# Where an exp tile is put: places chosen by the kernel's own order account, with new times for adding transfers

## The chip, the cores and the metric

The kernel runs on one core of a Trainium2 chip. The metric is the device time of one execution in microseconds (us), from launch to end, as the median of several runs. The profile is one further execution with the hardware profiler on; its span runs from the first to the last instruction.

## The reference, cut to what matters

Everything is float32. Eight images of 256 channels and 32 x 32 pixels go through three parts.

```python
# part 1: attention of 1024 pixel queries over 1426 pooled and convolved keys, 8 heads of 32
k_map, v_map = kv_w @ groupnorm(x)
ks, vs = layernorm(pooled(k_map)), layernorm(pooled(v_map))     # levels 32x32, 16x16, 11x11, 5x5
attn = softmax(q @ k.T * SCALE)
x = x + proj(mix(attn @ v))
# part 2: self-attention over the 1024 tokens, one head of 256
t = t + softmax(q @ k.T * SCALE) @ v
# part 3: eight experts of three 256 x 256 layers on every token, summed by gates
t = t + sum_e gate[e] * (relu(bn(relu(bn(n @ W1[e])) @ W2[e])) @ Wo[e] + bo[e])
```

In parts 1 and 2 the softmax is taken without a row maximum: exp of the scaled scores, the weighted values, the column sums, one division. A check at the end falls back to a slower path if a sum has left its bounds.

## The kernel before, in words

**Stages.** `attention` (L914) computes parts 1 and 2 together, `experts` (L2178) part 3. In the profiled execution the first lasts until about 1925 us. Within `experts` the order of the instructions is written out by hand, but for the gates. Within `attention` it comes from `Flow` (from L671): the kernel keeps an account of its own, with a clock for each engine (`now`), for each tile the time at which it is ready (`ready`) and last read (`read`), and costs by operation (`cost`, L724). Every instruction goes through `note` (L766), which ties it behind the last one written for its engine, so that the order in which Python writes the instructions is the order of each engine's queue. All instructions appear under line 671 in the profile, since they are issued through `Flow.Engine`.

**What is written when.** The main loop at the end of `attention` goes over 8 images, 2 channel halves, 2 query halves and 11 key chunks of 128 keys, 352 steps; the 12th chunk, of 18 keys, is handled once an image. A step writes `scores` (L1538) and then `values` (L1548) of the step before. All other work is in generators (`spawn`, L846), each with a rank, which yield what they need next: an engine and tiles. `step` (L883) resumes those for which `runnable` (L856) holds. For PE that is as long as there is credit, or as long as PE's clock is half a microsecond short of `until`, the time at which the scores' PSUM place becomes free by the account. DVE work is let in when DVE's clock is at most 4.0 us ahead of PE's if its tiles are ready, and otherwise when they will be ready within 1.5 us of PE's clock. `finish` (L896) resumes generators by the earliest start, whatever the credit, until a condition holds.

**The life of an exp tile.** `scores` writes 16 matmuls in the array's small tiles into the one PSUM tile `sc` (4 banks), takes a tile of the tag `pt` (128 x 4 x 512, 1 MiB; six places in SBUF), and writes one exp from `sc` to `pt`. `values` multiplies it with the values into `pv`. Of each two neighbouring chunks the odd exp tile is then added to the even one by an adding DMA that GpSimd (POOL) issues (`add`, L1593). The generator `sums` (L1600) adds each such pair to the first pair of its unit on DVE, in two halves, and at the end multiplies the first pair with ones for the column sums. So an odd tile's place is free when its add has landed, an even one's after the DVE sum, and the first pair's after the last matmul of the unit of 11 steps. Two of the six places serve the first image's maps (`first_maps`, L1198) at the start, and one the last image's input in `project` (L1631) at the end.

**Part 2's exp tiles** carry the tag `p1` (128 x 2 x 256, six places). `layer1` (L1695) writes four for each of the 32 query blocks, held back by the count `taken`; `outputs` (L1749) reads them. Small weight tiles in `mix` and `weights1` use the same tag earlier.

**Places before.** `Flow.tile` (L705) asks the tile framework for a tile of a tag with six places; which place it gets is up to the framework's scheduler. Beside it the account keeps a list of six names and replaces the one with the smallest `end`, the later of `ready` and `read` by the account. An instruction's start in the account includes the `ready` of the tile that it writes; a place's end from uses that are not written yet is not known to it.

**Transfers in the account.** `note` gives a DMA 1.0 us for the issue on POOL and 0.4 on another queue, and a landing by `transfer` (L814): a fixed part, its own work by size, and what is left of earlier transfers of its own and of the other queues.

```python
size = 4e-3 * out.shape[0] * out.free_size()          # thousand bytes
lag = self.transfer(engine, end, size * (0.0054 if engine == "POOL" or both else 0.003))
return 1.7 + left[mine] + min(left[mine], left[other]) + self.served - at
```

The functions that the change touches:

Of the kernel before, what the change touches and what calls it, by code (L numbers as in the profile page):

```python
# [8 lines left out]
F32 = mybir.dt.float32  # L9
# [7 lines left out]
P = 128  # L17
# [6 lines left out]
NK = 1426  # L24
# [10 lines left out]
MARGIN = 1.5  # L35
AHEAD = {"DVE": 4.0, "ACT": 2.0, "POOL": 1.0, "SP": 10.0}
NEAR = {"DVE": 1.5, "ACT": 2.0, "POOL": 1.0, "SP": 10.0}
BUFS = {"sm": 2, "sx": 1}
AHEAD3 = 3
PACE2 = 8.0  # L40
# [13 lines left out]
class Kit:  # L54
# [3 lines left out]
        self.nc = nc  # L58
        self.n = 0

    def tile(self, pool, shape, tag, bufs=None):
        self.n += 1
        return pool.tile(shape, F32, tag=tag, name=f"{tag}_{self.n}", bufs=bufs)

    def rstd(self, out, var, eps):
# [592 lines left out]
class Flow:  # L658
# [27 lines left out]
    def __init__(self, tc, kit):  # L686
        nc = tc.nc
        self.tc, self.kit = tc, kit
        self.now = dict.fromkeys(("PE", "DVE", "ACT", "POOL", "SP"), 0.0)
        self.last = {}  # L690
        self.ready, self.read, self.writer, self.reader, self.slots, self.open = {}, {}, {}, {}, {}, set()
        self.pe = self.Engine(self, "PE", nc.tensor)
        self.ve = self.Engine(self, "DVE", nc.vector)
        self.act = self.Engine(self, "ACT", nc.scalar)
        self.pool = self.Engine(self, "POOL", nc.gpsimd)
        self.sp = self.Engine(self, "SP", nc.sync)
        self.threads = []
        self.cut = {}
        self.also = {}
        self.tiled = None  # L700
        self.columns = False
        self.left, self.served = [0.0, 0.0], 0.0
        self.credit, self.port = [0.0, 0.0], 0.0

    def tile(self, pool, shape, tag, bufs=1):  # L705
        t = self.kit.tile(pool, shape, tag, bufs=bufs)
        slots = self.slots.setdefault(tag, [None] * bufs)
        i = min(range(bufs), key=lambda i: self.end(slots[i]))
        self.ready[t.name] = self.end(slots[i])
        slots[i] = t.name  # L710
        if tag in BUFS:
            self.open.add(t.name)
        return t

    def end(self, name):

# [49 lines left out]
    def note(self, engine, op, ins, args, kwargs):  # L766
        aps = [a for a in (*args, *kwargs.values()) if hasattr(a, "tensor") or hasattr(a, "space")]
        out = kwargs.get("out", args[0] if args else aps[0])
        srcs = [a for a in aps if a is not out]
        prev = self.last.get(engine)  # L770
        if prev is not None:
            self.tc.add_manual_dep(
                ins.ins,
                prev,
                mybir.DependencyInfo(mybir.DependencyClass.NoSync, mybir.DependencyReason.DATA),
                reason="program order",
            )
        self.last[engine] = ins.ins.name
        start = self.now[engine]
        names = [n for a in srcs for n in self.keys(a)]  # L780
        outs = self.keys(out)
        for n in (*names, *outs):
            if self.writer.get(n) != engine:
                start = max(start, self.ready.get(n, 0.0))
        for o in outs:
            if self.reader.get(o, engine) != engine:
                start = max(start, self.read.get(o, 0.0))
        cost = self.cost(engine, op, out, srcs)
        if engine == "PE":

            tiling = None if op == "transpose" else self.tiling(srcs)
            if tiling != self.tiled:
                cost += {None: 0.2, "rows": 0.2, "columns": 0.13, "both": 0.2}[tiling]
                self.tiled = tiling

        wide = [a for a in srcs if a.space != PSUM and a.free_size() > 4]
        if "dma" not in op and engine == "POOL" or engine == "DVE" and wide and (len(wide) > 1 or op in ("tensor_scalar", "tensor_copy")):
            start = max(start, self.port)
            self.port = start + cost
        self.now[engine] = end = start + cost  # L800
        lag = 0.15
        if "dma" in op:
            both = out.space == DRAM and srcs[0].space == DRAM
            size = 4e-3 * out.shape[0] * out.free_size() if out.space != DRAM else 4e-3 * srcs[0].shape[0] * srcs[0].free_size()
            lag = self.transfer(engine, end, size * (0.0054 if engine == "POOL" or both else 0.003))
        for n in {*outs, self.key(out)}:
            self.ready[n] = max(self.ready.get(n, 0.0), end + lag)
            self.writer[n] = "DMA" if "dma" in op else engine
        self.open.difference_update(names)
        for n in {*names, *map(self.key, srcs)}:  # L810
            self.read[n] = max(self.read.get(n, 0.0), end + lag)
            self.reader[n] = engine

    def transfer(self, queue, at, work):  # L814

        span = max(0.0, at - self.served)
        self.served = max(self.served, at)
        mine, other = queue == "POOL", queue != "POOL"
        left = self.left
        both = 2 * min(left)  # L820
        done = min(span, both) / 2
        for i in range(2):
            left[i] = max(0.0, left[i] - done - max(0.0, span - both))
        left[mine] += work
        return 1.7 + left[mine] + min(left[mine], left[other]) + self.served - at

    @staticmethod
    def key(a):
# [85 lines left out]
def attention(tc, kit, f, outer, ended, nb, consts, x, t1, t2, hn, bounds, vecs, q_t, kv_t, proj_t, gqk_t, wqk, wqkv, vecs1, w1_d, w1c, gate_d, wrc, vecs2, bnvec, w2_d, h2d, between, pre, held):  # L914
# [6 lines left out]
    with ExitStack() as ctx:  # L921
# [71 lines left out]
        def mix():  # L993
# [46 lines left out]
            yield act(wa)  # L1040
            f.act.activation(wa, wa, AF.Exp)
            yield ve(wa)
            rs = T(wp, [P, 2], "wars")
            f.ve.tensor_reduce(rs, wa, AX.X, ALU.add)
            f.ve.reciprocal(rs, rs)
# [18 lines left out]
            for c in range(2):  # L1064
                f.pe.matmul(
                    ps[:, c * C : (c + 1) * C], lhsT=bdt[:, c, :], rhs=pjw[:, c, :], start=True, stop=True
                )
            yield ve(ps)
            raw = T(l1, [P, 2, C], "s")
            f.ve.tensor_copy(raw, ps.rearrange("p (c q) -> p c q", c=2))  # L1070
            for c in range(2):
# [28 lines left out]
        def ve(*tiles):  # L1100
            return "DVE", tiles, None
# [76 lines left out]
            return dy, dx, max(0, -dy), n - max(0, dy), max(0, -dx), n - max(0, dx)  # L1178


        pmaps = [T(pool_, [P, NK], f"p{i}") for i, pool_ in enumerate((between, work))]
        for t in pmaps:
            f.split(t, 512, HW)
        first, large, whole, pooled, asked, halved = {}, [], [], [], [], []
# [67 lines left out]
        def first_keys(half):  # L1252
# [3 lines left out]
            for m in range(2):  # L1256
# [5 lines left out]
                for i, tap in enumerate((4, 0, 1, 2, 3, 5, 6, 7, 8)):  # L1262
# [7 lines left out]
                        stop=i == 8,  # L1270
                    )
                f.act.activation(acc[:, half * 512 : half * 512 + 512], ps, AF.Identity, bias=db(m, 0))
            large.append(("keys", half))

        def taps(c, s, p, acc, base=0):
# [324 lines left out]
        def sums(n, pairs):  # L1600

            for i in range(1, NKC // 2):
                yield until(lambda: len(pairs) > i)
                for j in range(0, 4, 2):
                    s = pairs[0][:, j : j + 2, :]
                    yield ve(s, pairs[i])
                    f.ve.tensor_tensor(s, s, pairs[i][:, j : j + 2, :], ALU.add)
            yield until(lambda: normalised[0] == n)
            yield pe(pairs[0], tag="sm")
            total = small()  # L1610
            for j in range(4):
                f.pe.matmul(
                    total[DH * j : DH * j + DH, :], lhsT=kit.ones[:, :DH], rhs=pairs[0][:, j, :], start=True, stop=True
                )
            return total

        def normalise(b, c, sl, total, n):
# [12 lines left out]

        def project(b):  # L1631
            if b == nb - 1:
                last = T(work, [P, 2, HW], "pt", bufs=6)
                f.sp.dma_start(last, x[b].rearrange("(k p) n -> p k n", p=P))
            for m in range(2):
# [17 lines left out]
                        f.pool.dma_start(out=t1[b][:, m, sl], in_=xt, accum_op=ALU.add)  # L1653
            if b == nb - 1:
                f.sp.dma_start(t1[b], last)
            projected[0] += 1

        def scale_tokens(src, n):
# [90 lines left out]
        def outputs():  # L1749

            for i in range(4 * nb):
# [23 lines left out]
                for m in range(2):  # L1775
                    for kc in range(8):
# [7 lines left out]
                            stop=kc == 7,  # L1784
                        )
                taken[0] += 1
                yield ve(ps, rec)
                m2 = ps.rearrange("p (m q) -> p m q", m=2)
                f.ve.tensor_tensor(m2, m2, rec[:, None, :].to_broadcast([P, 2, C]), ALU.mult)
# [31 lines left out]
        def weights1():  # L1821
# [76 lines left out]
            wrs = T(wp, [P, 2, NE], "wrs")  # L1898
            yield from centred(cm, wr, NE, wrs)
            f.sp.dma_start(wrc, wrs)  # L1900
            ready.append(True)

        gw, wv = (T(l1, [P, 2, C], tag) for tag in ("gw", "wv"))
# [4 lines left out]
        def experts_ahead():  # L1908

            yield until(lambda: made[0] == nb and key_parts[0] == 3 * nb)  # L1910
            for e, tag in enumerate(("p0", "kt")):
                w = held["w"][e] = T(between, [P, 2, 2, C], tag)
                f.sp.dma_start(w[:, 0], w1c[:, e])
                f.sp.dma_start(w[:, 1], w2_d[:, e])
# [78 lines left out]
        for i in range(len(steps) + 1):  # L1993
            if i < len(steps):
# [12 lines left out]
                if kc == NKC - 1:  # L2007
                    f.finish(lambda: key_parts[0] > 3 * b + 2 and (b, 1) in qs and (b or len(asked) == 4))
                    tail_scores(b)
                else:  # L2010
                    pts[i] = scores(b, c, sl, kc)
                f.step()
            if i and steps[i - 1][3] < NKC - 1:
# [7 lines left out]
                f.finish(lambda: kc1 // 4 in vts[b1])  # L2021
                values(b1, c1, kc1, pts[i - 1], pv)
                if kc1 % 2:
                    add(kc1, pts.pop(i - 1), pts[i - 2])
                    pairs.append(pts.pop(i - 2))
                if kc1 == NKC - 2:
# [725 lines left out]
```

## Time and profile before

| what | value |
|---|---|
| median of 3 runs | 3259.01 us (3258.67 to 3266.59) |
| profiled execution, its time | 3261.05 us |
| its span | 3259.2 us |
| mean granted PE clock | 0.98 |
| exps of part 1 on ACT | 352, 1877 ns each, 660.9 us |
| DVE sums of exp tiles | 320, 391.9 us busy |
| adding DMAs of 1 MiB | 160, 7.7 us from issue to landing (median) |
| adding DMAs of the last 18 keys | 32, 4.4 us |

The engines are PE (matmul), PEld (weight load, beside PE), DVE (VectorE), ACT (ScalarE), POOL (GpSimd) and SP (SyncE, which issues loads and stores). A row of the waits reads "who <- whom: us in total, times, longest"; where a transfer is named, the engine waited for its landing. A time line row gives start, length, engine, line, operation, output <- inputs, form and count, and in brackets how long the engine had been idle and what released it. Numbers are left out of tile names, so `pt` stands for every exp tile of part 1, and `p` for the maps as well as for `p1`. PEclk is the clock that PE was granted, as a share of full speed.

### The profile page before, as it was taken

How to read it: one execution, taken by the hardware profiler on the slowest of the kernel's cores; microseconds unless marked ns; L12 is line 12 of the kernel's file. 1: busy time of each engine (PE TensorE's matmuls, PEld its weight loads, DVE VectorE, ACT ScalarE, POOL GpSimd, SP SyncE). 2: the span in 40 equal slices, each digit the busy share in tenths (PEclk: the TensorE clock that was granted, in tenths of full speed). 3: DMA queues.
4: the chain of work that ended last, by engine and by line, in shares of the span. 5: the costliest groups of instructions: out<-in, count | busy, mean ns of one | idle time of the engine just before them, and what ended most of it. 6: DMA issues, size and time to landing. Idle time of an engine off the chain costs nothing.

```text
span 3259.2 us, 55911 instructions
## 1 busy us (share of the span) xinstructions
PE 3056.5 (94%) x22330; PEld 1789.3 (55%) x22330; DVE 2406.7 (74%) x4117; ACT 1682.6 (52%) x2301; POOL 1240.7 (38%) x1327
## 2 busy tenths in 40 slices
PE   8778799999979989989999999999999999999998
PEld 4322234334325334424333356777888888888887
DVE  5886786987877888969754544447888887777776
ACT  4566566666645657657665533333333334444443
POOL 3211413224222232232121112007655667777776
PEclk9899999999989999989999999999999999999999
DMA  1376657665664565565676645225444430000000
GB/s 54 86 153 156 125 124 155 137 148 111 141 145 84 128 151 113 137 143 111 141 182 126 144 111 207 94 88 171 146 149 149 149 117 20 20 20 33 20 14 21
DMA packets 115710, 368.68 MB, mean 113 GB/s; under 512 B 14305, under 2 KB 40233, under 8 KB 92209
## 3 DMA queue, kind: packets, MB, share of 16 engines
q0 software_dynamic: 28608, 179.85, 28.5%
q1 hardware_dynamic: 83472, 183.19, 16.7%
q8 instruction: 178, 2.92, 0.4%
q10 hardware_dynamic: 3360, 1.97, 0.2%
q14 instruction: 92, 0.75, 0.1%
HBM read 116.12 MB, written 83.40 MB: 61 GB/s over the span
## 4 chain that ended last, share of the span: by engine, by line
PE 49%; DVE 6%; DMA 3%; issue 2%; ACT 2%; POOL 1%; SPq 0%; DVEq 0%; POOLq 0%; ACTq 0%
PE bank L671 20%; PE y L671 10%; PE sm L671 9%; PE sx L671 4%; PE sc L671 3%; PE pv L671 3%; DVE h L671 2%; DMA pt<-pt 2%; ACT pt L671 1%; DVE acc L671 1%; DVE u L671 1%; DVE c L671 1%; DVE pt L671 1%; DVE t L671 0%; DMA t<-res 0%
## 5 line engine op out<-in xcount | busy, mean ns | idle before, releaser
L671 ACT ACTIVATE pt<-sc 128x2048 f32<-128x2048 f32 x352 | 660.9, 1877 | 296.7 <-PE sc L671 204.3
L671 DVE SCALAR_TENSOR_TENSOR acc<-p,vec,acc 128x961 f32<-128x961 f32 (+3 forms) x960 | 562.2, 594 | 35.1 <-ACT acc L671 9.4
L671 PE MATMUL sc<-q,kn 32*128 32x512 f32 (+1 forms) x3072 | 428.5, 662 | 125.1 <-ACT pt L671 121.8
L671 DVE TENSOR_TENSOR pt<-pt,pt 128x1024 f32<-128x1024 f32 x320 | 391.9, 1271 | 148.3 <-DMA pt<-pt 123.7
L671 PE MATMUL pv<-pt,vt 128*32 128x512 f32 x2816 | 390.9, 628 | 1.7 <-ACT vt L671 1.2
L671 ACT ACTIVATE h<-h,bnvec 128x512 f32<-128x512 f32 x450 | 340.4, 805 | 61.8 <-DVE h L671 53.1
L671 ACT ACTIVATE p1c<-bank 128x256 f32<-128x256 f32 x225 | 86.2, 383 | 553.5 <-PE bank L671 553.2
L671 POOL TENSOR_TENSOR rstd<-rstd,mhalf 128x4 f32<-128x4 f32 (+2 forms) x88 | 106.6, 1211 | 651.6 <-DVE rstd L671 560.2
L671 POOL DMA_DIRECT2D pt<-pt x160 | 146.3, 916 | 465.4 <-ACT pt L671 376.7
L671 DVE TENSOR_TENSOR h<-p1c,bank 128x512 f32<-128x512 f32 x225 | 153.3, 682 | 200.2 <-PE bank L671 196.5
L671 PEld LDWEIGHTS sc<-q,kn 32*128 32x128 f32 (+1 forms) x3072 | 115.7, 182 | 324.4 <-ACT pt L671 223.2
L671 POOL TENSOR_TENSOR tm<-h,tm 128x256 f32<-128x256 f32 x208 | 239.2, 1150 | 16.3
L671 DVE TENSOR_TENSOR h<-u,bank 128x256 f32<-128x256 f32 x450 | 229.2, 550 | 7.7
L671 PEld LDWEIGHTS pv<-pt,vt 128*32 128x32 f32 x2816 | 56.3, 109 | 281.3 <-issue 262.1
L671 POOL TENSOR_TENSOR tm<-h 128x512 f32<-128x512 f32 x104 | 133.2, 1281 | 202.6 <-ACT h L671 198.5
L671 DVE TENSOR_TENSOR h<-h,gate 128x1024 f32<-128x1024 f32 x128 | 199.9, 1561 | 0.5 <-ACT h L671 0.5
L671 PE MATMUL y<-t,s3e 128*128 128x256 f32 x768 | 187.0, 379 | 3.1 <-POOL t L671 1.7
L671 PE MATMUL bank<-t,s1e 128*128 128x256 f32 x726 | 178.1, 381 | 2.6 <-DVE t L671 2.4
L671 POOL TENSOR_TENSOR t<-h,t 128x256 f32<-128x256 f32 x214 | 169.5, 792 | 16.8
L671 POOL TENSOR_TENSOR t<-h 128x512 f32<-128x512 f32 x107 | 136.1, 1272 | 98.1 <-DVE h L671 77.4
L671 DVE TENSOR_TENSOR u<-h,bank 128x512 f32<-128x512 f32 x225 | 154.7, 688 | 24.7 <-PE bank L671 1.4
L671 PEld LDWEIGHTS y<-t,s3e 128*128 128x128 f32 x768 | 145.7, 190 | 24.0 <-POOL t L671 2.5
(376 smaller groups left out, 5557.5 us busy)
## 6 DMA issues: line engine op xcount, KB each, us to landing
pt<-pt POOLq DMA_DIRECT2D x160, 1024.0 KB, 7.7
h<-h SPq DMA_DIRECT2D x123, 512.0 KB
xi<-in_x_dram SPq DMA_DIRECT2D x16, 512.0 KB
t<-t SPq DMA_DIRECT2D x8, 1024.0 KB
res<-t SPq DMA_DIRECT2D x32, 256.0 KB
t<-res SPq DMA_DIRECT2D x32, 256.0 KB
hn<-res SPq DMA_DIRECT2D x32, 256.0 KB
hn<-hn SPq DMA_DIRECT2D x16, 512.0 KB
```

The lines of the kernel that those rows point to most:

```text
L671: ins = fn(*args, **kwargs)
```

## The change

Tiles of the tags `pt` and `p1` no longer come from one tag of six places but from six tags of one place each (`pt.0` to `pt.5`), and `Flow.tile` names the place. It takes the place with the smallest end among those whose tile isn't `held`. A tile is held from its making until `drop`, which stands where its last use has just been written (for an odd exp tile, just ahead of its add). Ahead of `scores` the main loop calls `finish` until a place of `pt` is not held (`vacant`); `project` waits for the same. The two maps `p0` and `p1` are renamed `map0` and `map1`, and nothing else changes for them. In the account the work of a transfer that POOL issues goes from 0.0054 to 0.0036 us per thousand bytes, and the fixed part of every transfer from 1.7 to 2.2 us. No instruction is added or taken away by the edits themselves, but the order in which the generators are resumed follows the account.

```diff
+OWN = {"pt", "p1"}
...
-    def tile(self, pool, shape, tag, bufs=None):
+    def tile(self, pool, shape, tag, bufs=None, slot=None):
         self.n += 1
+        if slot is not None:
+            return pool.tile(shape, F32, tag=f"{tag}.{slot}", name=f"{tag}_{self.n}", bufs=1)
...
     def tile(self, pool, shape, tag, bufs=1):
-        t = self.kit.tile(pool, shape, tag, bufs=bufs)
         slots = self.slots.setdefault(tag, [None] * bufs)
-        i = min(range(bufs), key=lambda i: self.end(slots[i]))
+        own = tag in OWN
+        i = min((i for i in range(bufs) if slots[i] not in self.held), key=lambda i: self.end(slots[i]))
+        t = self.kit.tile(pool, shape, tag, bufs=bufs, slot=i if own else None)
+        if own:
+            self.held.add(t.name)
         self.ready[t.name] = self.end(slots[i])
         slots[i] = t.name
...
+    def drop(self, *tiles):
+
+        self.held.difference_update(map(self.key, tiles))
+
+    def vacant(self, tag):
+        return any(name not in self.held for name in self.slots.get(tag, [None]))
...
-            lag = self.transfer(engine, end, size * (0.0054 if engine == "POOL" or both else 0.003))
+            lag = self.transfer(engine, end, size * (0.0036 if engine == "POOL" else 0.0054 if both else 0.003))
...
-        return 1.7 + left[mine] + min(left[mine], left[other]) + self.served - at
+        return 2.2 + left[mine] + min(left[mine], left[other]) + self.served - at
...
                     f.ve.tensor_tensor(s, s, pairs[i][:, j : j + 2, :], ALU.add)
+                f.drop(pairs[i])
...
+            f.drop(pairs[0])
             return total
...
+                    f.finish(lambda: f.vacant("pt"))
                     pts[i] = scores(b, c, sl, kc)
...
                 if kc1 % 2:
+                    f.drop(pts[i - 1])
                     add(kc1, pts.pop(i - 1), pts[i - 2])
```

Further `drop` calls of the same kind stand in `mix`, `first_keys`, `project`, `outputs` and `weights1`.

More of the change, by code (lines that the diff above doesn't have):

```diff
@@ L697, in __init__ @@
         self.threads = []
+        self.held = set()
         self.cut = {}
@@ L1042, in mix @@
             yield ve(wa)
+            f.drop(wk)
             rs = T(wp, [P, 2], "wars")
@@ L1068, in mix @@
             yield ve(ps)
+            f.drop(wa, pjw)
             raw = T(l1, [P, 2, C], "s")
@@ L1178, in windows @@
             return dy, dx, max(0, -dy), n - max(0, dy), max(0, -dx), n - max(0, dx)
-        pmaps = [T(pool_, [P, NK], f"p{i}") for i, pool_ in enumerate((between, work))]
+        pmaps = [T(pool_, [P, NK], f"map{i}") for i, pool_ in enumerate((between, work))]
         for t in pmaps:
@@ L1272, in first_keys @@
                 f.act.activation(acc[:, half * 512 : half * 512 + 512], ps, AF.Identity, bias=db(m, 0))
+                if ("keys", 1 - half) in large:
+                    f.drop(p)
             large.append(("keys", half))
@@ L1632, in project @@
             if b == nb - 1:
+                yield until(lambda: f.vacant("pt"))
                 last = T(work, [P, 2, HW], "pt", bufs=6)
@@ L1655, in project @@
                 f.sp.dma_start(t1[b], last)
+                f.drop(last)
             projected[0] += 1
@@ L1786, in outputs @@
                 taken[0] += 1
+                f.drop(*p1)
                 yield ve(ps, rec)
@@ L1900, in weights1 @@
             f.sp.dma_start(wrc, wrs)
+            f.drop(wvr, cm, g)
             ready.append(True)
@@ L1910, in experts_ahead @@
             yield until(lambda: made[0] == nb and key_parts[0] == 3 * nb)
-            for e, tag in enumerate(("p0", "kt")):
+            for e, tag in enumerate(("map0", "kt")):
                 w = held["w"][e] = T(between, [P, 2, 2, C], tag)
```

## The prediction

> **What bounds the kernel now.** I read the busy table and the slices first, then busy time by stage, then the waits of the two engines that pass exp tiles to each other, then the time lines of the worst places.
>
> The page, busy us and slices of 81.5 us:
>
> ```profile
> PE 3056.5 (94%) x22330; PEld 1789.3 (55%) x22330; DVE 2406.7 (74%) x4117; ACT 1682.6 (52%) x2301; POOL 1240.7 (38%) x1327
> ...
> PE   8778799999979989989999999999999999999998
> ...
> PEclk9899999999989999989999999999999999999999
> ```
>
> TensorE (PE) is the fullest engine, and of its dips (slices 1 to 5, 12, 15, 18) three stand beside dips of its granted clock (2, 12, 18). By stage, attention (with layer 1 in its gaps) and experts; columns are length, busy us and count of PE, PEld, DVE, ACT, POOL, then clock, DMA share, GB/s:
>
> ```profile
> 0.00:1925.00 1925.00, 1745.96 (x16493) 689.54 (x16494) 1448.84 (x2711) 1189.25 (x1481) 499.91 (x579) 0.97 0.60 131
> 1925.00:3259.00 1334.00, 1310.50 (x5839) 1099.77 (x5837) 957.89 (x1406) 493.31 (x821) 740.78 (x748) 1.00 0.26 88
> ```
>
> PE idles 1925 - 1746 = 179 us in attention and 23.5 us in the experts. The exp tiles live only in the first stage (last exp at 1898 us), so only there is anything to be won. Waits up to 1925 us, first of ACT, then of PE (total us, times, longest):
>
> ```profile
> ACT pt L671 <- PE sc L671: 204.3, 220, 2.5
> ACT pt L671 <- DMA pt<-pt: 71.7, 22, 7.3
> ```
>
> ```profile
> PE sc L671 <- ACT pt L671: 121.8, 99, 6.2
> ```
>
> The first ACT line is normal: the exp waits for its scores. The second isn't a data wait: an exp reads scores, never the result of an add. It waits because its place in SBUF is still being read by the adding transfer of an older exp. The PE line is the follow-on: scores have one PSUM place, so the next scores wait for the late exp. One such stretch, ACT in the time line (start, us, ..., [idle before <- releaser]):
>
> ```profile
> 655.33 1.88 ACT L671 ACTIVATE pt<-sc 128x2048 f32<-128x2048 f32 x1 [1.38 <-DMA pt<-pt]
> ...
> 664.24 1.88 ACT L671 ACTIVATE pt<-sc 128x2048 f32<-128x2048 f32 x1 [2.43 <-DMA pt<-pt]
> ...
> 680.48 1.88 ACT L671 ACTIVATE pt<-sc 128x2048 f32<-128x2048 f32 x1 [1.03 <-DMA pt<-pt]
> ```
>
> And the six stretches where such waits cluster, columns as above:
>
> ```profile
> 296.00:341.00 45.00, 31.53 (x192) 8.79 (x196) 23.58 (x49) 25.16 (x26) 14.27 (x16) 0.81 0.62 132
> 640.00:672.00 32.00, 25.00 (x184) 7.39 (x176) 27.61 (x65) 22.09 (x25) 10.94 (x11) 0.89 0.63 126
> 928.00:951.00 23.00, 11.13 (x64) 2.16 (x56) 14.39 (x17) 7.28 (x4) 2.85 (x3) 0.72 0.66 139
> 1172.00:1187.00 15.00, 7.50 (x32) 1.43 (x32) 9.97 (x17) 4.21 (x3) 0.86 (x1) 0.66 0.86 186
> 1405.00:1440.00 35.00, 27.98 (x166) 7.80 (x162) 20.68 (x32) 19.76 (x19) 17.37 (x19) 0.71 0.59 125
> 1448.00:1457.00 9.00, 5.06 (x36) 1.19 (x32) 7.25 (x16) 5.45 (x6) 1.96 (x3) 0.81 0.73 147
> ```
>
> In these 159 us PE is busy 108.2 and idle 50.8. Its busy time is also dear: at a clock of 0.81, busy x (1 - clock) is 31.53 x 0.19 = 6.0 us lost, and so on: 6.0 + 2.8 + 3.1 + 2.6 + 8.1 + 1.0 = 23.6. What place waits can have cost is thus about 50.8 + 23.6 = **74 us**, 2.3% of the span.
>
> **What the Trainium skill says.** "TensorE: Matmul & The Clock Gate", Part 1: The HAM clock gate, has the array fall to half clock after an idle window of about 3.4 us and stay so for at least one such window. The trace agrees: clocks of 0.66 to 0.89 stand just at these stalls, 1.00 between 400 and 600 us. So a stall is paid twice, and I price it so. "DMA: Bandwidth & Descriptors", Anatomy of one DMA, gives about 2.0 us plus bytes over 436 GB/s, an estimate of 4.4 us for 1024 KB; the adds differ, at 7.7 us median from issue:
>
> ```profile
> pt<-pt POOLq DMA_DIRECT2D x160, 1024.0 KB, 7.7
> ```
>
> The same page, Issuing engines are not separate DMA queues, says that all queues share 16 engines. The trace agrees: the add issued at 921.3 beside two x loads of 512 KB landed 11.3 us later, and the exp at 932.69 waited 6.83 us for it.
>
> **The change, part by part.**
>
> (1) Choice of place. I followed each of the six places through the trace, exp by exp, with the time of its last use. Of 352 exps some 30 waited for their place over 0.15 us. Ten of them had another place lying free: at 334.0, 339.6, 655.3, 664.2, 680.5, 962.1, 1186.5, 1218.0, 1450.5 and 1684.7 us, waits of 5.85 + 3.06 + 1.38 + 2.43 + 1.03 + 4.24 + 3.13 + 1.69 + 0.99 + 4.56 = 28.4 us. PE idle tied to these is 14.1 us (the rest was covered by other matmuls); their half clock adds 2.3 (at 334) + 2.8 (at 664) + 1.7 (at 1453) = 6.8. Three more (932.7, 1408.9, 1419.3) would have had a place 4.1, 1.0 and 4.1 us sooner; half of that reaching PE, with its clock, is 5. Sum 26 us if the account always picks the place that comes free first. It takes the longest free by its own times, and where the margin is 4 to 19 us, as in most of the ten, it need not be exact. I take three quarters: **-19 us** (bounds 0 and -26).
>
> (2) Waits that no choice removes. The other 20 (296 to 323, 876, 945, 1120, 1176, 1181, 1656 and smaller) had all six places in use. Left of the 74 us: about 48. Here the account itself changes. Before, it took the smallest end over all six places, those with unwritten uses too, whose end is then too early, so that it believed no exp ever waited. Now the place's end stands in the exp's start, the scores' PSUM place is seen free later, and `runnable` lets other matmuls in up to that time. A stall becomes filler, in idle and in clock, where filler is at hand and the account's end is near the true one. The second holds half way (it has 7.0 us for an add where 7.7 is measured), and the stretch at 296 to 341 comes before layer 1 gives much filler. I take 30%: **-14 us** (bounds 0 and -35).
>
> (3) The constants. An add of 1049 (thousand bytes) lands in the account 1.0 + 1.7 + 1049 x 0.0054 = 8.4 us after its issue; now 1.0 + 2.2 + 3.8 = 7.0. Measured: median 7.7, tail to 14.6. The DVE sum behind each is therefore written 1.4 us earlier into DVE's order and will stand about 7.7 - 7.0 = 0.7 us at the head of DVE's queue with data missing, 160 times: about 115 us more of DVE waiting over 1800 us. Behind it queue the taps of the maps, normalisation and layer norm pieces; who waits for those is PE's filler and, once a batch, the keys. DVE has 1925 - 1449 = 476 us of idle there, of which `pt` sums now stand for 141. I put **+6 us** on PE (bounds 0 and +25; the upper end is the second rival). Plain loads land 0.5 us later in the account: the consumers are written slightly later, which other work hides; 0.
>
> (4) `p1` the same way: no place wait of it shows among ACT's, since the test on `taken` holds the writer back; 0. `vacant`: in the order of the kernel before only two of 352 exps are written while all six places have a use to come, so it seldom forces anything; 0. No instruction is added or removed. Experts: their order is fixed by hand, so 0; matmuls drawn into attention come off the experts, which is why PE idle saved anywhere in attention counts in full.
>
> Sum: -19 - 14 + 6 = -27 us. The profiled execution took 3261.05 us (span 3259.2 and 1.9 around it): 3234. It lies 2 us above the median of the runs (3259.01), so against those: **3232 us**.
>
> **Rivals.**
> *The waits only move* (0.17): two thirds of the waiting exps found every place in use, and a place taken sooner leaves the next exp the later one. For it: the stretch at 1172 to 1187 has no free place at all, and adds there land after 12.3 and 14.6 us, which no constant covers. Against: at 664 one lay free for 11 us. It gives the sure part of (1) halved and the cost of (3): 3259 - 10 + 6 = 3255. The change not doing what it says (places held too long, so that fewer are used) ends here too.
>
> *DVE becomes the pace* (0.20), slower. In 1200 to 1400 us DVE is busy 174.6 of 200; with its share of today's `pt` waits (141 / 1900 x 200 = 15) and of the new ones (115 / 1850 x 200 = 12) it is full at 202. From that point the last taps of a batch come late, and all exps of the next batch wait for its keys. Price: some four adds run within a batch change, 4 x 0.7 = 3 us late, at seven changes 21 us: 3259 + 21 = 3280. Against: the neighbouring stretches have DVE at 161 to 166, and PE waits for `acc` just once now (7.1 us).
>
> **How the numbers follow.** Forecast 0.63 (3205 to 3249), moved waits 0.17 (3249 to 3266), DVE 0.20 (3262 to 3290). A measurement of this kernel tells about 0.3% (10 us) from no change: faster means below 3249, slower above 3269. Faster is 0.63 + 0.02; slower 0.16; the same 0.19. The range takes the upper bounds of (1) and (2) at the low end, 3259 - 26 - 35 + 6 = 3204, and at the high end the moved waits whole and the lower third of the DVE case: 3268.
>
> **What would show it.** Step 1: the ACT wait on DMA `pt<-pt` falls from 71.7 us to 30 to 45, and the waits at the ten times are gone. Step 2: PE's wait for ACT `pt` falls from 121.8 to about 95, and the clock from 0 to 1925 us rises from 0.97 to 0.98. Step 3: DVE's waits on `pt` transfers rise from 141 us to 180 or more. I am wrong if ACT's wait stays near 70, or if PE gets new waits for `acc`, `kn` or `kt`.

## The result, and the profile after

The changed kernel takes 3264.15 us (median of 12 runs, 3259.15 to 3271.39), the kernel before 3258.84 (12 runs). The ratio is 1.0011, interval 1.0003 to 1.0020: slower by about a tenth of a per cent, inside the 0.3% that the prediction called the same. Forecast was 3232 us. The profiled execution of the changed kernel has a span of 3269.4 us, so that some 5 us of its distance from before are its own.

The page's busy row and slices:

```profile
PE 3062.3 (94%) x22948; PEld 1773.0 (54%) x22948; DVE 2398.0 (73%) x4109; ACT 1676.3 (51%) x2293; POOL 1188.0 (36%) x1279
...
PE   8788899899899989999999999999999999999998
...
PEclk9898999999999999999999999999999999999999
```

The deep dips of PE at slices 12 and 18 have gone, and shallow ones stand at slices 8, 11 and 15, beside those of the first five. PE's counts here and before (22948 and 22330) are not to be compared, since a trace can lack some matmul records. Over the whole span PE idles 3269.4 - 3062.3 = 207 us; it was 203. The same stretch as before by stage (length, busy us and count of PE, PEld, DVE, ACT, POOL, then clock, DMA share, GB/s):

```profile
0.00:1925.00 1925.00, 1741.02 (x17118) 674.65 (x17118) 1448.89 (x2710) 1183.87 (x1475) 501.53 (x578) 0.97 0.60 131
```

What the forecast aimed at did happen. ACT's waits in that stretch, first for the scores, then for a place (adding transfer, DVE sum):

```profile
ACT pt L674 <- PE sc L674: 208.9, 213, 6.0
...
ACT pt L674 <- DMA pt<-pt: 9.6, 4, 3.6
...
ACT pt L674 <- DVE pt L674: 2.8, 3, 1.0
```

The place waits on transfers are 9.6 us where they were 71.7. PE's wait for the exp fell far less, from 121.8 us:

```profile
PE sc L674 <- ACT pt L674: 106.3, 92, 4.8
```

And this is what had come in their place. DVE's waits, of the kernel before and then of the changed one:

```profile
DVE pt L671 <- DMA pt<-pt: 123.7, 46, 14.9
...
DVE pt L671 <- DMA pt<-ptail: 17.6, 10, 3.8
```

```profile
DVE pt L674 <- DMA pt<-pt: 221.1, 81, 14.1
...
DVE pt L674 <- DMA pt<-ptail: 20.7, 13, 3.9
```

With the waits for the 18 last keys they grew from 141 to 242 us. How one of them reaches PE is seen in one stretch of the changed kernel's time line (start, us, engine, operation, [idle before <- releaser]):

```profile
462.06 0.86 POOL L674 DMA_DIRECT2D pt<-pt  x1 [5.29 <-ACT pt L674]
...
465.08 2.35 DVE L674 TENSOR_TENSOR pt<-pt,pt 128x1024 f32<-128x1024 f32 x2
...
467.61 1.14 PE L674 MATMUL sc<-q,kn 32*128 32x512 f32 x8
...
470.57 2.36 DVE L674 TENSOR_TENSOR pt<-pt,pt 128x1024 f32<-128x1024 f32 x2 [3.14 <-DMA pt<-pt]
472.85 1.75 DVE L674 RECIPROCAL rec<-sm 128x256 f32<-128x256 f32 x1
...
474.63 0.39 ACT L674 ACTIVATE sm<-rec 128x256 f32<-128x256 f32 x1 [5.24 <-DVE rec L674]
...
475.05 1.86 ACT L674 ACTIVATE pt<-sc 128x2048 f32<-128x2048 f32 x1
475.20 1.93 PE L674 MATMUL sm<-p,v 128*32 128x256 f32 x32 [3.23 <-ACT sm L674]
```

The add is issued at 462.1 and lands 8.4 us later, where the account counts 7.0 for an add with no other transfer under way. DVE has reached its sum at 467.4 and stands 3.1 us. Behind the sum in DVE's order is a reciprocal of layer 1, ready to go; ACT stands 5.2 us for it, since its copy for the bounds check is ahead of the next exp in ACT's order. The scores of that exp were written by about 468.7; it begins at 475.05. PE stands 3.2 us for the bank that ACT has not let go. This is one stretch. ACT's waits of this sort (`sm` and `sx` on DVE `rec`) rose in all from 69.2 + 36.5 = 106 us before to 145 us:

```profile
ACT sm L674 <- DVE rec L674: 94.1, 37, 5.5
...
ACT sx L674 <- DVE rec L674: 51.1, 16, 5.9
```

### The profile page after: what moved, and what is told of

The parts are those of the page before. It is cut to its first block, busy times and chain, and to the rows that moved or that the text cites. A ratio compares the mean times of both kernels' runs of the same rounds, so it can differ in the third digit from the quotient of the medians.

```text
span 3269.4 us, 57129 instructions
## 1 busy us (share of the span) xinstructions
PE 3062.3 (94%) x22948; PEld 1773.0 (54%) x22948; DVE 2398.0 (73%) x4109; ACT 1676.3 (51%) x2293; POOL 1188.0 (36%) x1279
## 5 line engine op out<-in xcount | busy, mean ns | idle before, releaser
L674 DVE SCALAR_TENSOR_TENSOR acc<-map,vec,acc 128x961 f32<-128x961 f32 (+3 forms) x960 | 554.8, 586 | 38.4 <-ACT acc L674 13.0
L674 ACT ACTIVATE h<-h,bnvec 128x512 f32<-128x512 f32 x434 | 328.2, 805 | 61.6 <-DVE h L674 54.2
L674 DVE TENSOR_TENSOR h<-u,bank 128x256 f32<-128x256 f32 (+1 forms) x434 | 220.9, 550 | 7.5
L674 POOL TENSOR_TENSOR tm<-h,tm 128x256 f32<-128x256 f32 x192 | 220.2, 1147 | 15.1
L674 POOL TENSOR_TENSOR tm<-h 128x512 f32<-128x512 f32 x96 | 123.0, 1281 | 185.8 <-ACT h L674 179.5
L674 PE MATMUL sm<-y,t 128*32 128x256 f32 (+1 forms) x2168 | 187.6, 379 | 2.2 <-DVE res L674 2.0
L674 POOL TENSOR_TENSOR t<-h 128x512 f32<-128x512 f32 x99 | 126.0, 1272 | 126.8 <-DVE h L674 95.8
L674 PE MATMUL bank<-h,w2e 128*128 128x256 f32 (+1 forms) x480 | 163.0, 469 | 2.6 <-DVE h L674 1.7
```

The lines of the kernel that those rows point to most:

```text
L674: ins = fn(*args, **kwargs)
```

## The experiments

The theory after the result (A): the places win what was forecast, and the shorter add time gives it back, because DVE's pair sums are written too early and stand at the head of DVE's queue. Its rivals: the place waits were only replaced by other lateness, whatever the times (B); any new order scatters, and there is no cause (C). In all, 18 kernels ran. "Waits" below are the whole of ACT's waits for a place (for the transfers, sums and matmuls that read a `pt` tile) and of DVE's for `pt` tiles, nearly all for transfers, as the view of the tile `pt` sums them: 81 and 141 us before, 15 and 242 after the change. They are those of one execution of a kernel, which can lie some way off its median (the change's 7 us above). Ratios are to the kernel before on the same chip.

**Each half alone.** Own places with the old times: `0.0054` and `1.7` put back into the changed kernel. New times with the framework's places: the same two numbers put into the kernel before.

> The changed kernel with the transfer times of before (0.0054 us per thousand bytes for POOL's transfers, 1.7 us fixed), so the choice of places alone. Theory A (the places win about 20 us and the shorter add time gives it away, because DVE's sums of exp tiles are written too early and stand at the head of DVE's queue): 3240 us +-8, DVE's waits on pt transfers back near 141 us from 242, ACT's waits on DMA pt<-pt still near 10. Theory B (the place waits were replaced by other lateness, whatever the times): 3262 +-6, with DVE's waits anywhere. Theory C (any new order scatters by 10 us either way): no relation to DVE's waits.

> The kernel before with the new transfer times (0.0036 and 2.2 us) and the places left to the framework. Theory A: slower, 3275 us +-8, DVE's waits on pt transfers near 240 us, ACT's place waits still 60 to 80 us. Theory B: 3259 +-6, since the times do little. Theory C: anywhere from 3249 to 3275.

Measured: places alone 3235.3 us, ratio 0.9923 [0.9909, 0.9938], waits 23 and 148. Times alone 3279.3, ratio 1.0062 [1.0047, 1.0076], waits 45 and 241. So the gain is real and the times take it away; B is out. The waits of the kernel with own places and old times, DVE's and ACT's:

```profile
DVE pt L674 <- DMA pt<-pt: 132.4, 50, 6.6
```

```profile
ACT pt L674 <- DMA pt<-pt: 11.7, 4, 5.0
ACT pt L674 <- DVE pt L674: 11.2, 3, 7.4
```

Place waits are nearly as low as in the change, DVE's near those of before. In times alone the place waits had nearly halved too, where I had expected 60 to 80 us of them, and the kernel was slower all the same. What does not differ is ACT's wait for `rec`, the path that the stretch at 467 us showed. In this kernel, 29 us faster than the change, it is the same 145 us:

```profile
ACT sm L674 <- DVE rec L674: 94.4, 37, 6.0
...
ACT sx L674 <- DVE rec L674: 51.0, 18, 6.9
```

So that path is real, but its sum doesn't tell the fast kernel from the slow one.

**The sums' place in DVE's order, alone.** In the changed kernel the account takes an add's result as ready for DVE 1.4 us later; in the kernel before, 1.4 us earlier. Nothing else differs by hand.

```diff
 def add(kc, pt, into):
     ...
+    f.ready[f.key(into)] += 1.4      # in the kernel before: -= 1.4
```

> The changed kernel, but the account takes the result of each exp tile's add as ready for DVE 1.4 us later, where the time of before put it; the places' ends and all other transfers keep the new times. Theory A: 3240 us +-8, since only the sums' place in DVE's order mattered, DVE's waits on pt transfers 130 to 160 us. Theory B: 3262 +-6. If it is the other transfers' 0.5 us that cost, it stays at 3262 though DVE's waits fall.

> The kernel before in everything, but the account takes the result of each exp tile's add as ready for DVE 1.4 us earlier, as the change does, with no other time and no place changed. Theory A: the whole cost of the change alone, 3276 us +-8, DVE's waits on pt transfers 220 us or more. If it is the other new times that cost (the 0.5 us of every load, the shorter queue of POOL's transfers): 3259 +-6. Theory C: anywhere.

Measured: later sums in the changed kernel 3234.2 us, ratio 0.9919 [0.9905, 0.9933], waits 21 and 184 (I had expected 130 to 160 for the second). That one line brings the whole gain of the places back, with all other new times in force, so with own places it isn't the 0.5 us of the loads. Earlier sums in the kernel before: 3248.5, ratio 0.9958 [0.9945, 0.9970], faster where I had expected 3276. Its waits tell why: DVE's rose to 221, as expected, but ACT's fell from 81 to 21, which I had left out. Early sums cost DVE and free places; where place waits are many, that can pay, though 14 us is less than the draws below move. It also means that the earlier sums alone don't explain times alone, 19 us slower than before: the 33 us between the two lie in the other new times or in the draw, and stay open.

**How long an add is in the account.** In the changed kernel 0.0036 is replaced by 0.0041, 0.0046, 0.0056 and 0.0066 us per thousand bytes, so that an add lands 7.5, 8.0, 9.1 and 10.1 us after its issue, and 0.0046 with the framework's places.

> The changed kernel with 0.0041 us per thousand bytes for POOL's transfers: an add lands 7.5 us after its issue in the account, between the change (7.0) and the fastest run (8.0). Theory A: between the two, 3240 us +-10, DVE's waits on pt transfers about 200 us. Theory C: anywhere from 3215 to 3270.

> The changed kernel with 0.0046 us per thousand bytes for POOL's transfers, so that an add lands 8.0 us after its issue in the account (7.0 in the change, 8.4 before, 7.7 measured). Theory A: most of the gain back, 3245 us +-8, DVE's waits on pt transfers about 170 us. Theory B: 3262 +-6.

> The changed kernel with 0.0056 us per thousand bytes for POOL's transfers: an add lands 9.1 us after its issue in the account. Theory A: DVE's waits on pt transfers fall on, to about 110 us, but places are believed free later than they are; 3225 us +-10. Theory C: 3215 to 3265 with no relation to DVE's waits.

> The changed kernel with 0.0066 us per thousand bytes for POOL's transfers: an add lands 10.1 us after its issue in the account, near the slowest tenth of those measured. Theory A: DVE's waits on pt transfers fall below 120 us, but sums and places are believed later than they are, so that place waits come back (over 27 us) or PE runs out of filler; 3200 to 3215 us. Theory C: 3205 to 3265.

> The kernel before, places left to the framework, with the transfer times of the fastest run so far (0.0046 us per thousand bytes for POOL, 2.2 us fixed: an add lands 8.0 us after its issue in the account). Theory A (places and the sums' place in DVE's order act apart and add up): about 24 us above the same times with own places, so 3240 us +-10, ACT's place waits 50 to 80 us. Theory C (every new order scatters, and the 3216 was a lucky draw): no relation, 3225 to 3275. If the times alone made the 3216: near 3220.

| landing in the account | us | ratio | waits ACT, DVE |
|---|---|---|---|
| 7.0 (the change) | 3264.2 | 1.0011 [1.0003, 1.0020] | 15, 242 |
| 7.5 | 3252.0 | 0.9967 [0.9955, 0.9980] | 19, 198 |
| 8.0 | 3215.8 | 0.9863 [0.9847, 0.9880] | 10, 176 |
| 9.1 | 3204.2 | 0.9819 [0.9806, 0.9831] | 29, 134 |
| 10.1 | 3248.2 | 0.9968 [0.9957, 0.9980] | 52, 111 |
| 8.0, framework's places | 3251.2 | 0.9963 [0.9950, 0.9976] | 54, 185 |

DVE's waits fall steadily with the time, ACT's place waits rise again at the end, and the best lies between. Own places with the old times, where an add lands after 8.4 us, stand among these with 3235.3 us and waits of 23 and 148. Each line is one order, though, and how far a redrawn order moves the time is seen below. My expectations were out by more than their margins in each: 3252, 3216 and 3204 us came for 3240 +-10, 3245 +-8 and 3225 +-10, and 3251 for 3240 +-10 with the framework's places. 10.1 us came out 33 us above the upper end that I had given it. In the trace of before the 160 landings lie from 6.9 us after issue, with a median of 7.7 and a slowest tenth above 10.1.

**DVE's dead time, with the order held.** One transpose into a scratch tile goes ahead of each of the 160 pair sums, and the account counts it as nothing. The order of every engine's other instructions is unchanged.

```diff
+    f.ve.transpose(stall, con[:, :512])      # once for each pair; cost 0.0 in the account
     f.ve.tensor_tensor(s, s, pairs[i][:, j : j + 2, :], ALU.add)
```

> The kernel with own places and 0.0056 us per thousand bytes (3204 us), plus one DVE transpose of 128 x 512 into a scratch tile ahead of each of the 160 pair sums, counted as nothing in the account: the order of all engines stays as it was, and DVE runs about 160 x 0.71 = 114 us of dead time at the very places where it waits for adds in the change. Theory A (a microsecond in which DVE stands at a sum costs PE about half of one, as a fit over the ten kernels says: 0.52): 3204 + 59 = 3263 us +-15. Theory C (what differs between the kernels is the order, and DVE's stalls are absorbed by its 25% of idle): 3204 to 3220.

> The same 160 dead transposes in the kernel before (3260 us), in its own order and with its own times. Theory A: 3260 + 59 = 3319 us +-15, less if the late sums are hidden by the place waits that stand beside them. Theory C: 3260 to 3276.

The groups of DVE in the first of them (count | busy us, mean ns | idle before and releasers):

```profile
L674 DVE TENSOR_TENSOR pt<-pt,pt 128x1024 f32<-128x1024 f32 x320 | 386.6, 1248 | 108.4 <-DMA pt<-pt 96.5 <-ACT pt L674 5.9 <-DMA pt<-ptail 5.8
...
L674 DVE STREAM_TRANSPOSE stall<-con 128x512 f32<-128x512 f32 x160 | 112.2, 701 | 0.0
```

112 us of dead time cost 3238.8 - 3204.2 = 35 us in the fast kernel (41 by the ratios, 0.9944 [0.9931, 0.9958] against 0.9819) and 3302.6 - 3260.1 = 43 us in the kernel before (1.0132 [1.0117, 1.0148]), where its place waits rose to 103 as well. A part of it only took the place of DVE's own waits, which fell from 134 to 108 and from 141 to 100. So a microsecond inserted costs 0.31 to 0.38: less than the 0.52 expected, and many times what a DVE with 476 us of idle time seemed to promise. Counted against what DVE's dead time grew by in the fast kernel, 112 - 26 = 86 us, it is 0.41 to 0.48. The change has 242 - 148 = 94 us more of DVE's waits than own places with the old times; at that price it would be 38 to 45 us slower, an estimate, and it measured 29, or 41 over the redrawn kernels below. C is out as the whole story, for the order was the same.

**The choice of place without the order.** In the changed kernel the account chooses as before, but the framework gives the place (`slot=None`); the order is the same on all engines.

> The changed kernel with the account's choice, times and order untouched on every engine, but the place of each tile given by the framework again. It parts the choice of place from the order that follows from it. If the choice itself is what removed the place waits: ACT's waits on pt transfers and sums rise from 12 us to 50 or more, and the time by 0.69 of that, to 3290 us +-10. If the waits went because the account now knows when places come free: 3264 us +-5 and waits near 12.

Measured: 3268.3 us, ratio 1.0028 [1.0016, 1.0039], waits 28 and 238. The account's own pick has 15 us of place waits where the framework's has 28, but in the two redrawn kernels of the change below, with the own pick, they are 25 and 23. In time the pick is worth about 5 us by the ratios; the two intervals overlap, so it may be nothing. I had expected 50 us of place waits or more if the pick were what removes them.

**How much is a draw?** The fixed part of a transfer is moved by 0.05 us: no cause moves by more than that, but every order is drawn anew.

> The changed kernel with 2.15 in place of 2.2 us for the fixed part of every transfer: no cause moves by more than 0.05 us, but the order of all engines is drawn anew. Theory A (DVE's stalls set the level): 3264 us +-12. Theory C (any new order scatters as widely as the kernels so far, 3204 to 3279): anywhere in there.

> The same with 2.25. Theory A: 3264 us +-12. Theory C: anywhere from 3204 to 3279.

> The kernel with own places and adds of 9.1 us in the account (3204 us), with 2.15 in place of 2.2 us for the fixed part. Theory A: 3204 us +-12, with 3215 likelier than 3204, since that was the fastest of many. Theory C: anywhere from 3204 to 3279.

> The same with 2.25. Theory A: 3204 us +-12 or somewhat above. Theory C: anywhere from 3204 to 3279.

> The kernel before with 1.75 in place of 1.7 us for the fixed part of every transfer: its order drawn anew, nothing else. If the 3260 us of before is a fair draw: 3260 us +-15. If it was a lucky one, as the choice among many versions would make it: 3270 to 3290.

> The kernel with own places and the transfer times of before, with 1.75 in place of 1.7 us. If the places' 25 us are a cause: 3235 us +-15, so at least 10 us under the redrawn kernel before. If they were a draw: near it.

| kernel | as it is | redrawn |
|---|---|---|
| before | 1 | 1.0008 [0.9994, 1.0022] |
| own places, old times | 0.9923 | 0.9897 [0.9881, 0.9914] |
| the change | 1.0011 | 1.0069 [1.0052, 1.0086], 1.0031 [1.0021, 1.0041] |
| own places, add at 9.1 us | 0.9819 | 0.9907 [0.9891, 0.9924], 0.9912 [0.9895, 0.9928] |

A draw moves the time by up to 0.9%, about 28 us. It moves the waits as well: at 9.1 us DVE's are 134 us in the first and 171 and 146 in the redrawn ones. The groups of this table stay apart: the kernels of the change don't come under before, those with own places and adds of 8.4 us (the old times) or 9.1 us in the account don't come near it. One of the change's, at 3281 us, lay above the 3264 +-12 that I had expected. And the 3204 us of the fastest was a lucky draw: the redrawn ones are at 3232, above the 3216 that I had allowed, the three average 0.9879, some 3220 us, and with so few draws that can't be told from own places with the old times, which average 0.9910.

**The same sum for all.** In all twenty traces, PE's busy time less what the half clock added to it (from the clock records) is 3005 to 3015 us. What differs is PE's idle and its half clock: 203 + 50 us before, 207 + 52 in the change, 184 + 38 with places alone, 159 + 40 in the fastest. So it isn't more work, though the order also decides in part which instructions run (4117 on DVE before, 4109 in the change). A fit over the eighteen kernels without dead time (ratios times 3259 us) gives 3134 us + 0.76 x ACT's place waits + 0.48 x DVE's `pt` waits, with standard errors of 0.19 and 0.09 and a residual of 13 us, within the size of a draw. For the change it says -66 x 0.76 + 101 x 0.48 = -50 + 48.

## Why the prediction was wrong

**What bounds the kernel: right.** PE's idle and its half clock in attention make up the differences, and the experts hide nothing: after 1925 us PE idles about 23 us before and after.

**Steps 1 and 2, place waits, -33 us together: right in sum, by luck in part.** Own places with the old times gave -25 and, redrawn, -34 us. The split was wrong as far as it was measured: I put -19 on the choice and -14 on the account's knowledge of when places come free. At the new times the pick itself is worth some 5 us, if anything; the order that follows from the account's own ends takes the place waits from 45 to 28, and the new times take them from 81 to 45 before that. With the old times the parts were not told apart. So the ten exps that I saw wait beside a free place were worth far less than I counted. That a place taken sooner is missing to the next exp, as the first rival has it, would explain this, but was not tested. The prediction also contradicts itself here: it counts the exp at 1186.5 us among the ten, and says that from 1172 to 1187 us no place was free.

**Step 3, the constants, +6 us: this failed.** The term's size in DVE came out right: I wrote "about 115 us more of DVE waiting", and it was 101. But I had it as 160 stands of 0.7 us, and the waits on adds went from 46 to 81, with 2.7 us each on average: fewer and longer, so that the agreement is luck in part. Its price on PE was wrong. I took DVE's 476 us of idle for a cover and put 6 of 115 on PE, 0.05 a microsecond; the dead transposes show 0.31 to 0.38. The whole step cost +29 us with own places and, by the averages of the redrawn kernels (1.0037 against 0.9910), +41 us, more than the upper bound of +25 that I had given it. With the framework's places it cost +19 us, though the earlier sums alone made that kernel 14 us faster. The cover was an average over the stage: it doesn't say whether DVE is idle where its work is waited for. I wrote that behind a sum stand taps, normalisation and layer norm pieces. At 467 us it was a reciprocal of layer 1, for which ACT, and behind ACT the next exp, stood in order. By which waits DVE's standing reaches PE in the whole kernel isn't shown: ACT's waits for `rec` are 145 us in the change and with own places alone, and PE's wait for the exp is 106 us in the change but 89 in one of its redrawn kernels, as with own places alone.

**The second rival** (0.20) named the right resource and the wrong mechanism: DVE did not fill up (1448.8 us busy before and 1448.9 after, up to 1925 us), nor did the keys come late (PE waited for `acc` on DVE 7.1 us before and 1.5 after, for `kt` on ACT 4.7 and 7.5). It was standing, not fullness, that cost. Its 3280 is near the redrawn 3281 and 3270, by another road.

**The checks given.** ACT's place waits were to fall to 30 to 45 us: 10. PE's wait for `pt` to about 95: 106. The clock to 0.98: it stayed at 0.97. DVE's waits to 180 or more: 242. Neither sign of being wrong came: ACT's wait didn't stay near 70, and PE got no new waits for `acc`, `kn` or `kt` that count. So the signs didn't cover the step that failed. DVE's waits were forecast, but their price was taken from DVE's idle sum, which doesn't say who waits behind a pair sum.

**Left open.** By which waits DVE's standing reaches PE; why one order is worth up to 28 us more than another with the same constants to 0.05 us; what the other new times do with the framework's places; and whether the 10.1 us kernel is slow for its place waits or by its draw.

## What to carry to other kernels

In an order that is planned ahead and kept by each engine's queue, a planned duration should not be near the fastest one but one that most transfers keep: planned at 7.0 us, adds of 7.7 to 10 us made the engine behind them stand for 242 us in all, planned at 8.0 or 9.1 for 176 and 134. Planned at 10.1 it stood for 111, but the place waits rose from 29 to 52 us and the time rose too; one order was measured there, so that end is open. A stall at the head of a queue isn't priced by that engine's share of idle time. Who waits for the instructions behind it shows where it can hurt; here its price came only from dead time put in with the order held. And a planner's constant is judged over several orders: a shift of 0.05 us, which means nothing, moved this kernel by up to 28 us.

## What the runs showed of the hardware

PE's clock fell to half without a long idle stretch. The page cited in the prediction (the Trainium skill, "TensorE: Matmul & The Clock Gate", Part 1: The HAM clock gate) has half clock follow an idle window of about 3.4 us. The traces agree only in part. Of the 21 stretches of half clock before, 6 had a gap of 3.4 us or more between matmuls in the 6.8 us ahead of them, and of the 23 in the changed kernel one had. In the changed kernel the half clock that began at 443.3 us followed 3.4 us in which PE was busy for 1.7 us, with no gap over 1.1 us in the 6.8 us before. So a few short stalls in a row were enough here, and the long ones that the change removed were not the only ones to cost clock: half clock cost 50 us before and 52 us after. What exactly brings it isn't settled, since one stretch in each trace (at 2183.8 us before, 2238.7 after) began with PE busy throughout. All this goes by the ends of matmuls as the profile models them.
